# A hand-made planner for 32 graph batches: other landing times for tiles turned by DMA, and new seeds for its order

## The chip, the cores and the metric

The kernel runs on one core of one Trainium2 chip. The metric is the device time in microseconds (us) of one execution of the whole program; the median of several executions counts. The engines are called TensorE (PE; its weight loads are PEld), VectorE (DVE), ScalarE (ACT), GpSimd (POOL) and SyncE (SP). In this kernel SP issues all transfers.

## The reference

64 graphs of 256 nodes with 128 features, fp32, share one 256 x 256 matrix `adj`. Four layers follow each other; each is `x = layernorm(x + f(x))`:

```python
# layer 0, five times; in_matrix = out_matrix = adj
m  = adj @ h;  av = concat([m, m])
z  = sigmoid(av @ w3.T + w3_b + u3)         # u3 = h @ u3_w.T + u3_b
r  = sigmoid(av @ w4.T + w4_b + u3)
hv = tanh(av @ w5.T + w5_b + (r * h) @ u5.T + u5_b)
h  = (1 - z) * h + z * hv
# layer 1: A = masked softmax of edge values, split in diagonal and rest
out = (A * I) @ (x @ W0) + (A * (1 - I)) @ (x @ W1) + bias
# layer 2: attention scores s_src[i] + s_dst[j], leaky, masked by adj, softmax;
#          (attn * adj) @ h, layernorm, relu; then adj @ h_gat, two dense layers, relu
# layer 3: x, adj x, adj^2 x, adj^3 x, each times a weight, twice, summed
```

## The kernel before

**Work.** The 64 graphs go in 32 pairs (`n_pairs`). A pair's state is one tile of 128 partitions x 512 values (2 graphs x 2 halves of the nodes x 128). Each pair passes `layer0`, `layer1`, `layer2` and `layer3`; many pairs are under way at once. `spread7` multiplies by the adjacency with seven block products in place of eight, so that TensorE saves one in eight and VectorE and GpSimd make the sums (L632 to L647). Everything is fp32.

**Turning tiles.** A product needs its left factor transposed. Most tiles are turned by transfers and not by TensorE (`turn`, L559): VectorE transposes 32 x 32 blocks (L576); SP writes the tile to a scratch buffer in DRAM (L578, tile class E, 256 KB); four transfers bring it back with the blocks exchanged (L584, 64 KB each). `wide_turn` (L589 to L598) does the same with longer runs for the last step of layer 0. In `layer2` a line of scores is written to DRAM (L851) and read back to all partitions (L852). In layer 0 the tile `h` is turned after each of the five steps: L760 (candidate), L763 (tanh), L764, L765, L767 (new state), L576, L578, L584, then `spread7`'s sums (L632) and products (L626).

**Order.** The order of every queue is worked out by a planner in the kernel's own text, `Schedule`, at build time. Each operation is entered with `S.add`: the engines that can do it with a price in us each, what it reads and writes, and for a transfer a triple `dma = (wait, move, after)`. `order` (L162) is a list scheduler: of all ready operations it takes the one that can start first; ties go to the smaller due time `late`. It gives it the engine that would end first, and a tile of its class (`CLASSES`; 38 of A, 8 of E, 8 PSUM banks). For a transfer the modelled pipe moves on, and its result is seen `after` later:

```python
if op.dma:
    wait, move, after = op.dma
    moved = max(moved, end + wait) + move * MARGIN
    seen = moved + after - end + LAG
```

`Op.seen` (L110) also uses the sum of the triple, and with it `rest` and the due time. The emitted order is fixed; on the chip each engine goes through its queue in order, and semaphores hold an instruction until what it needs is there. A read of a turned tile at the head of SP's queue waits there for its write, and the transfers behind it wait with it.

**Seeds.** The time of the plan is cut into windows of 15 us (`WINDOW`). `SEEDS` has one whole number for each. Other than 0, it adds a small pseudo-random amount to the due times of all operations in that window (L188 to L191), and so decides between operations that could start at the same time.

**Buffers and last pairs.** Tiles come free when the planner reckons their last user done; the same landing times go into that (L216 to L220). The last pairs are planned with shorter due distances (`LAST_DUE`) and with more work on TensorE (`PLAIN`, `BY_DMA`), since fewer pairs are left to fill gaps.

Of the kernel before, what the change touches and what calls it, by code (L numbers as in the profile page):

```python
# [12 lines left out]
P = 128  # L13
# [45 lines left out]

XLOAD, TLOAD = (0.6, 1.33, 2.5), (0.6, 1.05, 1.5)  # L60

SEEDS = [0, 93, 322, 1448, 7531, 11255, 17694, 0, 22928, 0, 31333, 39097, 43244, 44818, 49258, 57598, 58877,
         63429, 68827, 73007, 78086, 84417, 87701, 93086, 94151, 102956, 104573, 109816, 0, 116864, 121863,
         126231, 131449, 135312, 139647, 0, 151536, 152814, 156731, 164059, 167161, 172217, 176318, 180425,
         187172, 188269, 195902, 197063, 202029, 208186, 213802, 218747, 223086, 224899, 230352, 233509, 240645,
         242828, 250716, 251650, 259527, 0, 0, 0, 0, 0, 283015, 0, 295474, 0, 0, 0, 0, 314335, 0, 322518, 0,
         333851, 338782, 340488, 345007, 350633, 356967, 37123594, 37124702, 37129757, 37131905, 37136837,
         37140404, 37142955, 37148792, 37152814, 37156664, 37159159, 37162334, 37167804, 37170295, 37173551, 0]


def mm(cols, n=1):
# [42 lines left out]
class Schedule:  # L114
# [47 lines left out]
    def order(self, tiles):  # L162
# [9 lines left out]
        while ready:  # L172
            best, homes, seed = None, {}, SEEDS[window] if window < len(SEEDS) else 0
            for op in ready:
# [64 lines left out]
def kernel(ctx: ExitStack, tc: tile.TileContext, x, xT, adj, adjT, mats, cols, rows, out):  # L239
    nc = tc.nc  # L240
# [5 lines left out]
    S = Schedule(n_pairs)  # L246
# [4 lines left out]
    def pe(us, fn, r, w):  # L251
        S.add([("PE", us, fn)], r, w)
# [4 lines left out]
    def dve(us, fn, r, w):  # L257
        S.add([("DVE", us, fn)], r, w)
# [11 lines left out]
    def evacuate(o, i, r, w, us=(0.49, 0.61)):  # L270

        S.add([("ACT", us[0], lambda: nc.scalar.copy(o(), i())),  # L272
               ("DVE", us[1], lambda: nc.vector.tensor_copy(o(), i()))], r, w)
# [271 lines left out]
    def tokens(v):  # L545
        return v.at(4, D)
# [6 lines left out]
    def by_dma(site):  # L553
        return S.pair < n_pairs - BY_DMA[site]
# [4 lines left out]
    def turn(i, name, site, n=512):  # L559


        o = Value("A", name=name) if n == 512 else i
        if not by_dma(site):
            ts = [Value("PS", name="ps") for _ in range(n // 512)]
            for k, t in enumerate(ts):
                def fn(k=k, t=t):
                    for c in range(4):
                        nc.tensor.transpose(tokens(t)[:, c, :], i.at(n // P, P)[:, 4 * k + c, :], ident.ap)
                pe(TURN, fn, [i, ident], [t])
            for k, t in enumerate(ts):  # L570
                evacuate(lambda k=k: o.at(n)[:, 512 * k:512 * k + 512], lambda t=t: t.at(512), [t], [o])
            return o
        st, d = Value("A" if n == 512 else "B", name="turn"), Value("E", name="turn")
        if site == "y":
            return wide_turn(i, st, d, o)
        dve(n / 512 * 0.55 + 0.09, lambda: nc.vector.transpose(st.at(n), i.at(n)), [i], [st])  # L576
        blocks = lambda *ap: bass.AP(tensor=d.ap.tensor, offset=d.ap.offset, ap=ap)
        S.add([("SP", 0.52, lambda: nc.sync.dma_start(blocks([P, P], [P * P, n // P], [1, P]), st.at(n // P, P)))],  # L578
              [st], [d], (0.6, n / 512 * 0.86, 0.5))

        def move():
            for q in range(4):
                b = blocks([P, 32], [32 * P, n // 32], [1, 32])
                nc.sync.dma_start(o.at(n // 32, 32)[32 * q:32 * q + 32],  # L584
                                  bass.AP(tensor=b.tensor, offset=b.offset + 32 * q, ap=b.ap))
        S.add([("SP", 2.1 if n == 512 else 2.7, move)], [d], [o], (-0.8, n / 512 * 1.5, 0.9))
        return o

    def wide_turn(i, st, d, o):  # L589

        line = lambda start, *ap: bass.AP(tensor=d.ap.tensor, offset=d.ap.offset + start, ap=ap)
        dve(0.64, lambda: nc.vector.transpose(st.at(4, 4, 32).rearrange("p q c e -> p c q e"), i.at(4, 4, 32)), [i], [st])
        S.add([("SP", 0.52, lambda: nc.sync.dma_start(line(0, [512, P], [1, 512]), st.at(512)))], [st], [d], (0.6, 0.63, 0.5))

        def move():
            for q in range(4):
                nc.sync.dma_start(o.at(4, P)[32 * q:32 * q + 32], line(P * q, [512, 32], [512 * 32, 4], [1, P]))
        S.add([("SP", 2.1, move)], [d], [o], (-0.8, 1.23, 0.9))  # L598
        o.turned = True
        return o  # L600

# [135 lines left out]
    def layer0(x0, hT):  # L737
        h = x0
        for s in range(STEPS):
# [18 lines left out]
            def candidate(t=t, mT=mT, r=r):  # L758
# [9 lines left out]
                new.at(512), t.at(512), 0.5, hT.at(512), op0=ALU.mult, op1=ALU.add), [t, hT], [new])  # L768
            hT = new
            h = turn(hT, "h", "h" if s < STEPS - 1 else "y")  # L770
        y = Value("A", name="y")
        halves = lambda v: v.at(4, 4, 32).rearrange("p s c e -> p c s e") if v.turned else v.at(4, 4, 32)
# [14 lines left out]
    def layer1b(x1):  # L787
        xT = turn(x1, "xT", "x1")
        xb, rr = Value("A", name="xb"), Value("A", name="rr")
        dve_or_pool(lambda e: e.tensor_add(tokens(xb), tokens(x1), row("l1_bias", 4)), [x1, rbc], [xb])  # L790
        ts = []
        for i in range(2):
            t = bank()

            def fn(i=i, t=t):
                for b in range(2):
                    nc.tensor.matmul(t.at(2, 2, D)[:, :, b, :], tokens(xT)[:, 2 * b + i, :], W1.ap[:, i_w:i_w + 2, :], start=(b == 0),  # L797
                                     stop=(b == 1), skip_group_check=True)
            pe(mm(256, 2), fn, [xT, W1], [t])
            evacuate(lambda i=i: rr.at(2, N)[:, i], lambda t=t: t.at(512)[:, N:], [t], [rr], (0.28, 0.34))  # L800
            part = lambda t=t: t.at(2, 2, D)[:, 0]
            dve(0.335, lambda i=i, part=part: nc.vector.scalar_tensor_tensor(
                part(), part(), dcol.ap[:, i:i + 1], xb.at(2, 2, D)[:, :, i, :], op0=ALU.mult, op1=ALU.add), [t, dcol, xb], [t])
            ts.append(t)
        for i, t in enumerate(ts):
            def fn(i=i, t=t):
                for j in range(2):
                    nc.tensor.matmul(t.at(512)[:, :N], offT.ap[:, j, i * P:(i + 1) * P], rr.at(2, N)[:, j],
                                     start=False, stop=(j == 1), skip_group_check=True)
            pe(mm(256, 2), fn, [offT, rr, t], [t])  # L810
        s, rs = scale_stats([(t, range(i, 4, 2)) for i, t in enumerate(ts)])
        for i, t in enumerate(ts):
            scale_tokens(t, x1, range(i, 4, 2), s, rs)

    def layer1(x1):
        if plain("q1"):
            return layer1b(x1)
        qT = spread7(x1, offT, offT7)
        xb = Value("A", name="xb")
        xd = Value("A", name="xd")  # L820
        dc = lambda: dcol.ap[:, None, :, None].to_broadcast([P, 2, 2, D])

        def scaled():
            for c in range(4):
                nc.scalar.mul(tokens(xd)[:, c, :], tokens(x1)[:, c, :], dcol.ap[:, c % 2:c % 2 + 1])
        S.add([("ACT", 1.26, scaled), ("DVE+", TT, lambda: nc.vector.tensor_mul(xd.at(2, 2, D), x1.at(2, 2, D), dc())),
               ("POOL", 1.235, lambda: nc.gpsimd.tensor_mul(xd.at(2, 2, D), x1.at(2, 2, D), dc()))], [x1, dcol], [xd])
        dT = turn(xd, "dT", "x1")
        dve_or_pool(lambda e: e.tensor_add(tokens(xb), tokens(x1), row("l1_bias", 4)), [x1, rbc], [xb])
        t = seed((0.49, 0.61), tokens, lambda: tokens(xb), [xb, qT, dT])  # L830
        scale_norm(products([qT, dT], [lambda: mat("l1w1"), lambda: mat("l1w0")], t), x1)

    def layer2(x2):
# [13 lines left out]
        srow, d, sd = Value("A", name="row"), Value("D", name="line"), Value("A", name="sd")  # L847
        u, s = Value("B", name="u"), Value("S", name="nm")
        line = lambda *ap: bass.AP(tensor=d.ap.tensor, offset=d.ap.offset, ap=ap)
        dve(0.25, lambda: nc.vector.transpose(srow.at(4, 32), hs()[:, :, D - 30:D + 2]), [h], [srow])  # L850
        S.add([("SP", 0.52, lambda: nc.sync.dma_start(line([32, 4], [P, 4], [1, 32]), srow.at(4, 32)[31::32]))], [srow], [d], (0.5, 0.1, 0.5))  # L851
        S.add([("SP", 0.52, lambda: nc.sync.dma_start(sd.at(512), line([0, P], [1, 512])))], [d], [sd], (0.9, 0.7, 1.2))  # L852

        nm, den = (lambda k=k: s.at(32)[:, 4 * k:4 * k + 4] for k in range(2))
        d2v = Value("S", name="d2")
# [278 lines left out]
```

## Time and profile before

| | |
|---|---|
| median of 3 runs | 1471.28 us (1470.71 to 1473.59) |
| the profiled execution: its time | 1470.14 us |
| its span, first to last instruction | 1468.4 us |
| mean granted TensorE clock | 0.999 |
| bytes read from HBM, written | 118.43 MB, 99.42 MB |
| transfers `e<-a` / `a<-e` (turned tiles) | 283 of 256 KB / 1132 of 64 KB |
| transfers `e<-b` / `b<-e` (attention weights) | 32 of 512 KB / 128 of 128 KB |

The page gives busy times and shares of the span, the busy share in 40 slices, the transfers, and the chain of work that ended last. A row of waits reads: the engine and line that waited, on whom, us in total, how often, the longest. A row of windows gives the stretch, its length, the busy us of PE, PEld, DVE, ACT and POOL (with the number of instructions), the clock, the share of time in which the DMA engines were busy, and GB/s. Tiles are named by class: `a` is a working tile in SBUF, `e` the scratch tile in DRAM, `ps` a PSUM bank.

### The profile page before, as it was taken

To read this page: it belongs to the slowest core of one execution; us is meant where nothing else is said; L and a number is where in the kernel's file an instruction comes from. 1 tells how busy PE (TensorE), PEld (TensorE's weight loads), DVE (VectorE), ACT (ScalarE), POOL (GpSimd) and SP (SyncE) were. 2 spreads that over 40 slices of the span, in tenths; PEclk is the share of its full clock that TensorE was granted. 3 is DMA by queue.
4 is the path that set the end of the run, shared out by engine and by line. 5 is a ranking of instruction groups with operands and counts; after the bars stand their busy time and mean duration, and the time that the engine had idled before them with its cause. 6 is when DMAs were issued, how large, how long until landed. Compare 5 with 4: busy or idle time off the path is not lost.

```text
span 1468.4 us, 29406 instructions
## 1 busy us (share of the span) xinstructions
PE 1457.9 (99%) x8188; PEld 1064.4 (72%) x8188; DVE 1270.8 (87%) x3161; ACT 1071.2 (73%) x3291; POOL 1005.7 (68%) x1551
## 2 busy tenths in 40 slices
PE   9999999999999999999999999999999999999998
PEld 6565666666677778777767777777777766788998
DVE  7877788888899999988888888888888999999995
ACT  3444555677788888778776778676786887789986
POOL 4532554566777889878766776777778786877664
PEclk9999999999999999999999999999999999999999
DMA  7553555767788988786767687676777695877773
GB/s 228 123 107 71 125 127 121 147 147 153 159 164 164 192 186 165 160 171 145 145 146 151 159 166 148 138 165 127 167 156 156 142 180 121 166 169 167 156 141 73
DMA packets 901284, 219.84 MB, mean 150 GB/s; under 512 B 673280, under 2 KB 892544, under 8 KB 901120
## 3 DMA queue, kind: packets, MB, share of 16 engines
q1 hardware_dynamic: 901120, 217.96, 71.1%
q8 instruction: 66, 1.08, 0.3%
q14 instruction: 98, 0.80, 0.2%
HBM read 118.43 MB, written 99.42 MB: 148 GB/s over the span
## 4 chain that ended last, share of the span: by engine, by line
PE 95%; DVE 2%; DMA 1%; ACT 1%; SPq 0%; issue 0%; POOL 0%; POOLq 0%; DVEq 0%; ACTq 0%
PE ps L626 24%; PE ps L744 9%; PE ps L745 9%; PE ps L752 9%; PE ps L759 9%; PE ps L760 9%; PE ps L782 7%; PE ps L1012 6%; PE ps L882 4%; PE ps L1055 2%; PE ps L842 2%; PE ps L608 2%; PE ps L1038 1%; PE ps L797 0%; DMA W<-mats_in 0%; SPq L584 0%
## 5 line engine op out<-in xcount | busy, mean ns | idle before, releaser
L626 PEld LDWEIGHTS ps<-aT,a 128*128 128x128 f32 x2192 | 296.4, 192 | 85.1 <-issue 74.8
L272 ACT COPY a<-ps 128x512 f32<-128x512 f32 (+2 forms) x610 | 255.1, 438 | 109.7 <-PE ps L626 53.1
L626 PE MATMUL ps<-aT,a 128*128 128x128 f32 x2192 | 321.3, 275 | 0.7 <-DVE a L632 0.7
L748 ACT ACTIVATE a<-ps,bzrh 128x512 f32<-128x512 f32 x160 | 110.5, 691 | 98.7 <-PE ps L745 94.7
L763 ACT ACTIVATE ps<-ps,bzrh 128x512 f32<-128x512 f32 x160 | 106.4, 665 | 96.6 <-PE ps L760 94.3
L759 PE MATMUL ps<-a,w 128*128 128x512 f32 x320 | 163.8, 593 | 0.0
L745 PE MATMUL ps<-a,w 128*128 128x512 f32 x320 | 163.4, 592 | 0.0
L760 PE MATMUL ps<-a,u5h 128*128 128x512 f32 x320 | 163.4, 592 | 0.0
L752 PE MATMUL ps<-a,w 128*128 128x512 f32 x320 | 163.3, 594 | 0.1
L647 DVE TENSOR_TENSOR a<-ps,a 128x256 f32<-128x256 f32 x237 | 98.5, 418 | 73.8 <-ACT a L272 50.5
L641 POOL TENSOR_TENSOR a<-a 128x256 f32<-128x256 f32 x125 | 93.1, 748 | 97.7 <-ACT a L272 96.7
L705 ACT ACTIVATE a<-ps 128x128 f32<-128x128 f32 x498 | 132.0, 289 | 36.2 <-PE ps L782 16.0
L713 POOL TENSOR_TENSOR s<-s,neg_half 128x4 f32<-128x4 f32 x127 | 140.2, 1105 | 6.8
L645 POOL TENSOR_TENSOR a<-a 128x128 f32<-128x128 f32 x204 | 100.6, 497 | 62.9 <-DVE a L641 52.9
L782 PEld LDWEIGHTS ps<-W,a 128*128 128x128 f32 x960 | 124.0, 192 | 18.0 <-issue 15.1
L754 ACT ACTIVATE a<-ps,bzrh 128x512 f32<-128x512 f32 x160 | 110.4, 692 | 36.4 <-PE ps L752 30.5
L782 PE MATMUL ps<-W,a 128*128 128x128 f32 x960 | 135.0, 275 | 0.0
L744 PE MATMUL ps<-a,W 128*128 128x512 f32 x256 | 131.0, 593 | 0.4 <-DVE a L647 0.4
L576 DVE STREAM_TRANSPOSE a<-a 128x512 f32<-128x512 f32 x185 | 128.3, 697 | 2.8 <-ACT a L705 0.5
L745 PEld LDWEIGHTS ps<-a,w 128*128 128x128 f32 x320 | 60.8, 190 | 76.5 <-issue 68.6
L760 PEld LDWEIGHTS ps<-a,u5h 128*128 128x128 f32 x320 | 60.8, 190 | 76.5 <-issue 64.8
L725 ACT ACTIVATE a<-ps,s 128x128 f32<-128x128 f32 x362 | 109.0, 388 | 5.0 <-POOL s L713 3.5
(266 smaller groups left out, 3612.7 us busy)
## 6 DMA issues: line engine op xcount, KB each, us to landing
e<-a SPq DMA_DIRECT2D x283, 256.0 KB
a<-e SPq DMA_DIRECT2D x1132, 64.0 KB
e<-b SPq DMA_DIRECT2D x32, 512.0 KB
b<-e SPq DMA_DIRECT2D x128, 128.0 KB
x<-x_in SPq DMA_DIRECT2D x32, 256.0 KB
t<-xT_in SPq DMA_DIRECT2D x32, 256.0 KB
a<-d SPq DMA_DIRECT2D x32, 256.0 KB
y_out<-a SPq DMA_DIRECT2D x31, 256.0 KB
```

The source lines that it names most:

```text
L272: S.add([("ACT", us[0], lambda: nc.scalar.copy(o(), i())), ("DVE", us[1], lambda: nc.vector.tensor_copy(o(), i()))], r, w)
L576: dve(n / 512 * 0.55 + 0.09, lambda: nc.vector.transpose(st.at(n), i.at(n)), [i], [st])
L626: pe(mm(128), lambda: nc.tensor.matmul(blk(t, k), left(), rt(), start=start, stop=True, skip_group_check=True), [*r, right, terms, *[t] * ...
L705: nc.scalar.activation(tokens(junk)[:, c, :], v.at(len(tiles), D)[:, k, :], AF.Square, scale=D ** -0.5, accum_out=mv()[:, c, 1:2])
L713: pool(1.02, lambda: nc.gpsimd.tensor_tensor(rs(), rs(), neg_half.ap, op=ALU.pow), [s, neg_half], [s])
L744: nc.tensor.matmul(t.at(512), mat("u3"), hT.at(512), start=True, stop=False)
L745: nc.tensor.matmul(t.at(512), w4.ap, mT.at(512), start=False, stop=True)
L748: act(0.59, lambda t=t, r=r: nc.scalar.activation(r.at(512), t.at(512), AF.Tanh, bias=bzrh.ap[:, 1:2], scale=0.5), [t, bzrh], [r])
L752: pe(mm(512), lambda t=t, mT=mT: nc.tensor.matmul(t.at(512), w3.ap, mT.at(512), start=False, stop=True, skip_group_check=True), [w3, mT, t ...
L759: nc.tensor.matmul(t.at(512), w5.ap, mT.at(512), start=True, stop=False)
L760: nc.tensor.matmul(t.at(512), u5h.ap, r.at(512), start=False, stop=True)
L782: nc.tensor.matmul(tokens(t)[:, c, :], tokens(i)[:, c, :], w(), start=(first and k == c == 0), stop=(k == len(lefts) - 1), skip_group_chec ...
```

## The change

The landing times of the turned tiles become four numbers of one tuple, all larger than before, and the table of seeds is a new one. No operation, engine choice or price is edited otherwise.

```diff
+SLOW = (1.3, 1.1, 1.4, 0.8)
+
-SEEDS = [0, 93, 322, 1448, 7531, 11255, 17694, 0, 22928, 0, 31333, 39097, 43244, 44818, 49258, 57598, 58877,
...
+SEEDS = [0, 113, 303, 1481, 0, 12107, 0, 23552, 32642, 38944, 40117, 45598, 51141, 55839, 63359, 69543, 72829,
...
         S.add([("SP", 0.52, lambda: nc.sync.dma_start(blocks([P, P], [P * P, n // P], [1, P]), st.at(n // P, P)))],
-              [st], [d], (0.6, n / 512 * 0.86, 0.5))
+              [st], [d], (0.6, n / 512 * 0.86, SLOW[0]))
...
-        S.add([("SP", 2.1 if n == 512 else 2.7, move)], [d], [o], (-0.8, n / 512 * 1.5, 0.9))
+        S.add([("SP", 2.1 if n == 512 else 2.7, move)], [d], [o], (-0.8, n / 512 * 1.5, SLOW[1]))
...
-        S.add([("SP", 0.52, lambda: nc.sync.dma_start(line(0, [512, P], [1, 512]), st.at(512)))], [st], [d], (0.6, 0.63, 0.5))
+        S.add([("SP", 0.52, lambda: nc.sync.dma_start(line(0, [512, P], [1, 512]), st.at(512)))], [st], [d], (0.6, 0.63, SLOW[0]))
...
-        S.add([("SP", 2.1, move)], [d], [o], (-0.8, 1.23, 0.9))
+        S.add([("SP", 2.1, move)], [d], [o], (-0.8, 1.23, SLOW[1]))
...
-        S.add([("SP", 0.52, lambda: nc.sync.dma_start(line([32, 4], [P, 4], [1, 32]), srow.at(4, 32)[31::32]))], [srow], [d], (0.5, 0.1, 0.5))
-        S.add([("SP", 0.52, lambda: nc.sync.dma_start(sd.at(512), line([0, P], [1, 512])))], [d], [sd], (0.9, 0.7, 1.2))
+        S.add([("SP", 0.52, lambda: nc.sync.dma_start(line([32, 4], [P, 4], [1, 32]), srow.at(4, 32)[31::32]))], [srow], [d], (0.5, 0.1, SLOW[3]))
+        S.add([("SP", 0.52, lambda: nc.sync.dma_start(sd.at(512), line([0, P], [1, 512])))], [d], [sd], (0.9, 0.7, SLOW[2]))
```

Since the planner works the whole order out anew from these numbers, the queues of all engines differ from about the 28th microsecond of TensorE's work on; the first 44 operations of TensorE and its last 15 are the same. Lines of the kernel after are two higher than before from `SLOW` on.

## The prediction

> **What bounds the kernel now.** I read the page first (shares, slices, chain), then the waits of TensorE, then windows of the late stage, then what SP's queue waits for.
>
> The page:
>
> ```profile
> span 1468.4 us, 29406 instructions
> PE 1457.9 (99%) x8188; PEld 1064.4 (72%) x8188; DVE 1270.8 (87%) x3161; ACT 1071.2 (73%) x3291; POOL 1005.7 (68%) x1551
> ...
> DVE  7877788888899999988888888888888999999995
> ...
> q1 hardware_dynamic: 901120, 217.96, 71.1%
> ...
> PE 95%; DVE 2%; DMA 1%; ACT 1%; SPq 0%; issue 0%; POOL 0%; POOLq 0%; DVEq 0%; ACTq 0%
> ```
>
> TensorE is busy 99% and is 95% of the chain that ended last. The other 5% of the chain is not idle TensorE: the chain passes through other engines while TensorE still works off its queue. What TensorE itself waited for, in the view of waits:
>
> ```profile
> PE ps L1012 <- DVE a L901: 1.4, 1, 1.4
> PE ps L332 <- DVE ones L330: 1.2, 1, 1.2
> PE ps L842 <- DMA a<-e: 0.8, 1, 0.8
> PE ps L626 <- DVE a L632: 0.7, 1, 0.7
> PE ps L808 <- DVE ps L802: 0.4, 1, 0.4
> PE ps L744 <- DVE a L647: 0.4, 1, 0.4
> PE ps L1012 <- ACT x L725: 0.2, 1, 0.2
> ```
>
> Seven stops, each once, 5.1 us in all. Only one ends with a DMA. By the timeline the 1.2 and the 0.7 belong to the start; the other five lie at 1193, 1304, 1326, 1357 and 1368 us. The windows say the same (us, PE, PEld, DVE, ACT, POOL, clock, DMA share, GB/s):
>
> ```profile
> 12.00:480.00 468.00, 468.00 (x2214) 304.01 (x2213) 393.51 (x870) 294.36 (x754) 264.81 (x417) 1.00 0.65 139
> 480.00:1160.00 680.00, 680.00 (x3959) 500.68 (x3959) 596.24 (x1512) 522.97 (x1626) 515.72 (x797) 1.00 0.75 156
> 1160.00:1200.00 40.00, 39.50 (x269) 32.18 (x268) 37.67 (x93) 30.49 (x107) 32.40 (x48) 1.00 0.91 173
> 1280.00:1320.00 40.00, 39.16 (x246) 31.57 (x245) 36.05 (x96) 33.98 (x123) 31.33 (x48) 1.00 0.71 155
> 1320.00:1360.00 40.00, 39.39 (x277) 35.25 (x276) 39.76 (x123) 36.81 (x147) 32.28 (x47) 1.00 0.75 163
> 1360.00:1400.00 40.00, 38.52 (x276) 36.29 (x275) 37.54 (x118) 36.49 (x149) 26.98 (x37) 1.00 0.77 165
> ```
>
> For 1148 us TensorE never stops; later it loses bits where VectorE is at 90 to 99%.
>
> A busy PE need not be at its pitch, so I priced it. In the timeline 128-column matmuls start 0.112 us apart (16 in 1.79), 256-column ones 0.216, 512-column ones 0.429. The records hold 6028 + 256 of the first kind (130 columns with them), some 290 of the second, 1600 of the third: 704 + 63 + 686 = 1453 us. So 15 us of the span are not matmul at pitch: about 4.6 up to the 12th us, 5.3 after the last matmul starts (1463.1), and 5.2 between. Those 5.2 are the 3.2 that the waits show, about 0.26 hidden in each of five stops (a matmul is drawn 0.275 long and starts 0.112 apart, and the first after a stop is 0.1 late), and two short gaps that only the chain shows (1171, 1370 us).
>
> What SP's queue waits for:
>
> ```profile
> SPq L578 <- DVE a L576: 142.0, 83, 8.0
> SPq L584 <- DMA e<-a: 115.9, 83, 4.7
> ...
> SPq L597 <- DMA e<-a: 21.9, 17, 2.9
> SPq L584 <- DMA e<-b: 18.0, 12, 3.2
> ...
> SPq L852 <- DMA d<-a: 3.7, 4, 1.1
> ```
>
> A read of a turned tile waits at the head of SP for its write 112 times, 156 us in all; every later transfer stands behind it. That is what the change works on.
>
> [...]
>
> **The change part by part.** No instruction of TensorE or SP is added or removed: 4110 matmuls as the program issues them (the fp32 ones appear as two in the records) and the same 1744 transfers, shape by shape. So the 1453 us and the 218 MB stay. Three things move.
>
> (a) *The planner's landings.* Write 0.5 to 1.3, read 0.9 to 1.1, line write 0.5 to 0.8, line read 1.2 to 1.4 us. They change only when an operation counts as ready. In the two orders, of 347 write/read pairs, those with nothing between on SP go from 39 to 19, one operation 106 to 88, two 94 to 114, three 55 to 73; the mean from 2.11 to 2.28. A filler read issues four transfers at about 0.49 (L584), 2 us of cover. Twenty pairs out of zero, at the 1.4 us of a mean wait (115.9/83), is some 28 us less waiting of SP, a fifth of 156. Its worth for the end: what TensorE loses to transfers, 0.83 + 0.26 = 1.1 us at 1304. Nothing else, since TensorE's own queue covers the rest.
>
> (b) *Room on TensorE.* Counting matmuls at pitch between the one a turned h hangs on (L760) and the first that needs it (L626): least 13.1 us before, 13.7 after; twentieth part 14.5 and 15.4; median 21.8 and 24.4. The chain itself is 0.665 + 0.688 + 0.684 + 0.678 + 0.697 (L763 to L576) + 2.8 landing of the write + three issues at 0.49 + 4.3 of the last read = 12.0. The tightest gain 0.6 us. Before 1160 us this is worth nothing.
>
> (c) *New seeds reshuffle everything from the 28th us on.* By counts, VectorE gets 11 more 128x512 TENSOR_TENSOR (0.69 us each), 5 more 128x256 (0.42), 4 more 128x512 scalar forms (0.5), and gives up 4 statistics pairs (0.4), 2 copies, some small ones: +8 us. ScalarE loses 16 128x128 (0.4) and 4 512-wide (0.6): -8. GpSimd loses 11 128x512 (1.3) and gains 6 128x256 (0.75) and 3 128x128 (0.5): -8. Spread over the span these cost nothing under TensorE; beside its last 300 us VectorE has as many operations in the planner's list (553 before, 555 after). In the stage where TensorE's work passes from 1320 to 1360 us, GpSimd goes from 46 operations to 54 (two L710/L713 pairs at 1.39, five at 0.75, less one at 0.5): 32.3 + 6.0 = 38.3 of 40 us, while VectorE falls from 86 to 79. That is a bottleneck exchanged for another: bounded below by -1.15 (what TensorE loses there now: 0.19 + 0.42 + two hidden parts) and above by +6 if all of GpSimd's addition shows. I take +0.6, since GpSimd still fits and VectorE is relieved. The start (first 44 operations of TensorE) and the last 15 are the same, so 4.6 and 5.3 stay.
>
> Sum: 1468.4 - 1.1 (a) + 0.6 (c), other late gaps taken as exchanged one for one = 1467.9. The profiled execution took 1470.14, 1.7 more than its span; the median is 1471.28, 1.1 above that. So 1470.8.
>
> **Rivals.**
> *Likeliest: same within 0.2%* (0.2% is 2.9 us, about what a measurement can tell). TensorE's late idle stays between 2.5 and 8 us: 1468.5 to 1474. For it: pitch, unchanged matmuls, 1148 us without a stop. Against: all late stops are chance meetings of queues and are drawn anew. Chance 0.44.
> *Transfers were behind the late stops too.* The stops that end at VectorE would go back to tiles that landed late, and the new room would remove nearly all 5.2: 1471.28 - 4.5 = 1466.8. For it: DMA share 0.91 at 1160, 14 stops of GpSimd's L632 at a<-e (26.8 us). Against: four of five end at VectorE or ScalarE, 90 to 99% busy. No version of this order can get below 1466. Chance 0.20.
> *Slower: the late crowd.* Place: 1320 to 1400 us, the last 14 batches ending together. Price: GpSimd's +6.0 us of work in a stage with 7.7 us of room; its L713 lies in each normalisation, nothing else can run it, and L705/L725 on ScalarE and then TensorE wait. It decides once GpSimd's queue passes 40 us of work in 40, so with 1.7 us of waits on top; then 1471.28 + 5 = 1476. For it: VectorE was at 39.76 of 40 there. Chance 0.28.
> *The change doesn't do what it says*: delayed reads push loads and later writes back, SP (1004 issues of L584's small reads alone take 0.487 us each, 489 us) meets the same waits elsewhere, and several late tiles come 2 to 4 us late: 1480. For it: fillers load the DMA engines in between. Against: distances grew on average. Chance 0.08.
>
> **How the numbers follow.** Faster by over 0.2% 0.20, within 0.44, slower 0.36. Range: from 1466.8, the floor of the second case, to 1478, past the crowd; outside stay most of the last case and a bad crowd. The likeliest one's own range is 1468.5 to 1474.
>
> **What would show it.** (a) right: L584 and L597 waiting for e<-a and e<-b fall from 156 to about 125 us and no TensorE stop ends with a DMA. (b) right: no TensorE stop from 12 to 1160 us. (c) right: late windows lose 2 to 8 us of TensorE; GpSimd near 38 us at 1320. The forecast is wrong if windows before 1160 show TensorE under full, or if TensorE's late idle is under 2 or over 8 us.

## The result, and the profile after

The kernel after takes 1468.98 us (median of 19, 1468.22 to 1470.28), the kernel before beside it 1471.15 (median of 19, 1469.49 to 1473.59): ratio 0.9985, 95% interval 0.9978 to 0.9992. That is 2.2 us or 0.15% less: real by the interval, and inside the 0.2% that was called no change.

The page of after (busy us, share of the span, instructions; then the transfers):

```profile
span 1468.5 us, 29324 instructions
PE 1458.2 (99%) x8188; PEld 1064.8 (73%) x8188; DVE 1277.1 (87%) x3166; ACT 1067.8 (73%) x3277; POOL 990.8 (67%) x1549
...
q1 hardware_dynamic: 901120, 217.96, 70.9%
```

TensorE is as full as before. VectorE has 6.3 us more work, ScalarE 3.4 and GpSimd 14.9 less. What TensorE waited for, after:

```profile
PE ps L1014 <- POOL a L634: 1.6, 1, 1.6
PE ps L628 <- DVE a L634: 1.3, 2, 0.7
PE ps L334 <- DVE ones L332: 1.2, 1, 1.2
PE ps L746 <- DVE a L649: 0.5, 1, 0.5
PE ps L628 <- DMA a<-e: 0.3, 1, 0.3
```

4.9 us in place of 5.1, in other places. The windows of after (PE, PEld, DVE, ACT, POOL busy) answer to those of before:

```profile
480.00:1160.00 680.00, 678.58 (x3978) 502.19 (x3977) 606.11 (x1524) 522.17 (x1631) 507.63 (x786) 1.00 0.77 158
1160.00:1200.00 40.00, 39.90 (x205) 26.96 (x204) 38.03 (x94) 32.50 (x91) 25.85 (x43) 1.00 0.77 152
...
1280.00:1320.00 40.00, 40.00 (x266) 32.14 (x265) 36.63 (x99) 36.45 (x124) 33.65 (x50) 1.00 0.84 165
1320.00:1360.00 40.00, 39.94 (x281) 35.97 (x280) 38.85 (x122) 37.62 (x153) 37.34 (x53) 1.00 0.76 167
1360.00:1400.00 40.00, 38.35 (x272) 36.04 (x271) 37.04 (x116) 36.84 (x144) 28.07 (x37) 1.00 0.79 156
```

From 1160 us on TensorE now loses 1.8 us where it lost 3.4; but it loses 1.4 between 480 and 1160, where before lost nothing. So the two profiled spans are level (1468.4 and 1468.5), and the 2.2 us of the medians are not to be seen in this pair of profiles: before's profiled execution (1470.14 us) was quicker than 16 of the 19 times of before, and after's (1470.28 us) was the slowest of its 19.

What did change plainly is SP's queue. Its waits for the writes of turned tiles and of the score line, after:

```profile
SPq L586 <- DMA e<-a: 52.3, 39, 3.5
...
SPq L586 <- DMA e<-b: 15.3, 9, 3.3
...
SPq L599 <- DMA e<-a: 12.1, 6, 3.9
...
SPq L854 <- DMA d<-a: 8.6, 8, 2.3
```

88 us in 62 waits, against 160 us in 116 before.

### The profile page after: what moved, and what is told of

It reads as the page before. It is cut to its first block, busy times and chain, and to the rows that moved or that the text cites. A ratio compares the mean times of both kernels' runs of the same rounds, so it can differ in the third digit from the quotient of the medians.

```text
span 1468.5 us, 29324 instructions
## 1 busy us (share of the span) xinstructions
PE 1458.2 (99%) x8188; PEld 1064.8 (73%) x8188; DVE 1277.1 (87%) x3166; ACT 1067.8 (73%) x3277; POOL 990.8 (67%) x1549
## 4 chain that ended last, share of the span: by engine, by line
PE 94%; DVE 2%; POOL 2%; SPq 1%; issue 1%; DMA 0%; ACT 0%; POOLq 0%; DVEq 0%; ACTq 0%
PE ps L628 24%; PE ps L761 9%; PE ps L746 9%; PE ps L762 9%; PE ps L747 9%; PE ps L754 9%; PE ps L784 7%; PE ps L1014 6%; PE ps L884 4%; PE ps L1057 2%; PE ps L844 2%; PE ps L610 1%; PE ps L1040 1%; SPq L586 1%; PE ps L799 0%
## 5 line engine op out<-in xcount | busy, mean ns | idle before, releaser
L274 ACT COPY a<-ps 128x128 f32<-128x128 f32 (+2 forms) x612 | 255.7, 437 | 112.0 <-PE ps L628 52.2
L643 POOL TENSOR_TENSOR a<-a 128x256 f32<-128x256 f32 x139 | 107.2, 774 | 93.1 <-ACT a L274 90.4
L746 PE MATMUL ps<-a,W 128*128 128x512 f32 x256 | 131.1, 594 | 0.5 <-DVE a L649 0.5
L767 DVE SCALAR_TENSOR_TENSOR ps<-a,ps 128x512 f32<-128x512 f32 x160 | 109.2, 683 | 3.8 <-ACT a L756 2.8
```

The source lines that it names most:

```text
L274: S.add([("ACT", us[0], lambda: nc.scalar.copy(o(), i())), ("DVE", us[1], lambda: nc.vector.tensor_copy(o(), i()))], r, w)
L746: nc.tensor.matmul(t.at(512), mat("u3"), hT.at(512), start=True, stop=False)
```

## The experiments

Twelve kernels, in three sets. Two questions: did the landing times bring the 2.2 us, or the new seeds; and do TensorE's stops hang on transfers at all? Where the kernel before is given beside a set, it ran on the same chip.

**Landings and seeds apart** (e1 to e4).

```diff
 e1: -SLOW = (1.3, 1.1, 1.4, 0.8)
     +SLOW = (0.5, 0.9, 1.2, 0.5)      # seeds of after kept
 e2: seeds of before, SLOW of after
 e3: SLOW as in e1,  SEEDS = [0]
 e4: SLOW of after,  SEEDS = [0]
```

> The landing times of before with the seeds of after. If the landings themselves bring the gain, this is at the time of before, 1471 us or a little more. If the new seeds bring it, it is at 1469. If a table of seeds only fits the landings it was made with, it is above both kernels, 1473 or more, and SP waits for its writes about 160 us as before.

> The landing times of after with the seeds of before. Landings: 1469 us, with SP's waits for writes near 90 us. Seeds: 1471. A misfit of the two: 1473 or more, though SP's waits fall all the same.

> No seeds at all, landing times of before. By the landings theory this is slower than its partner with the landing times of after by 2 us or more. By the seeds theory both are the same and both slower than the seeded kernels by several us (1473 to 1485).

> No seeds, landing times of after. Landings theory: 2 us or more below the partner with the landing times of before. Seeds theory: level with it, 1473 to 1485. In both, SP waits for writes about half as long as in the partner.

Measured, beside a before of 1470.86: e1 1507.46 (ratio 1.0244, 1.0230 to 1.0258), e2 1500.94 (1.0207, 1.0193 to 1.0221), e3 1505.79 (1.0244, 1.0227 to 1.0262), e4 1496.68 (1.0174, 1.0160 to 1.0188).

All four are 26 to 37 us slower than the kernel before. I had expected a misfit to cost 2 us; it costs as much as having no seeds at all. A table of seeds is worth its 2% only with the landing times that it stands beside; by the planner's text, other landing times change what is ready at each moment, so that a window begins from another state. The planner's own reckoning shows the loss too: worked out again from the kernels' text, its plan (`self.span`) ends at 1481 us for before and 1482 for after, but between 1513 and 1540 for e1 to e4, e11 and e12. So these orders are worse already as plans. (Among the six, and between before and after, the plan's end doesn't rank the measured times.) The change can't be divided into "landings" and "seeds" by these runs; it is a pair exchanged for a pair. Without fitting seeds the larger landings look worth 9 us (e3 to e4), and 6.5 across e1 and e2. The last set tests that.

Where e3 and e4 lose their time (stretches 12 to 1280, 1280 to 1440 us, and 1440 us to the end of the span at 1503.8 and 1495.7; columns as above), first e3, then e4:

```profile
12.00:1280.00 1268.00, 1260.45 (x6812) 886.65 (x6811) 1116.32 (x2636) 885.19 (x2600) 851.09 (x1345) 1.00 0.71 148
1280.00:1440.00 160.00, 153.81 (x1020) 134.21 (x1019) 142.45 (x429) 128.19 (x485) 123.87 (x184) 0.98 0.80 155
1440.00:1520.00 80.00, 47.59 (x326) 44.16 (x324) 32.34 (x95) 32.56 (x135) 23.45 (x37) 0.90 0.23 50
```

```profile
12.00:1280.00 1268.00, 1262.75 (x6769) 883.81 (x6768) 1105.21 (x2606) 870.67 (x2539) 859.37 (x1352) 1.00 0.71 147
1280.00:1440.00 160.00, 146.97 (x1002) 130.16 (x1001) 144.13 (x433) 138.41 (x554) 123.59 (x177) 0.98 0.80 162
1440.00:1520.00 80.00, 50.18 (x387) 48.21 (x385) 33.04 (x96) 38.97 (x155) 29.26 (x47) 0.98 0.22 50
```

In 1268 us TensorE loses 8 us (e3) and 5 (e4); in the next 160 alone 6 and 13; after 1440 us e3 loses 16 more and e4 5.5. In the kernel before these stretches lose 0.5, 3 and 5 us. So most of the idle time that these two orders add lies in the last part, where few pairs are left. The rest of their loss, 14 and 12 us, is drawn as busy: 1461.9 and 1459.9 us in these stretches, against 1447.9 in before.

**Profiles again, and reads that wait for nothing** (e5 to e8).

```diff
 e5, e6: no edit
 e7 (of before), e8 (of after):
+        cold = x.offset + S.pair % 16 * 131072
-                                  bass.AP(tensor=b.tensor, offset=b.offset + 32 * q, ap=b.ap))
+                                  bass.AP(tensor=x.tensor, offset=cold + 32 * q, ap=b.ap))
...
```

> A second profile of the kernel before. In its first one the span was 1468.4 us, as short as that of after (1468.5), while the medians differ by 2.2 us. If the first profile was a lucky execution, this one shows TensorE stops that the first had not, ending with transfers (landings theory) or with VectorE and ScalarE (chance meetings), 1 to 4 us more in all.

> A second profile of the kernel after, whose first profile was the longest of its 19 times. A span of about 1467 us is expected, with the stops of 558 and 570 us smaller or gone if they were chance, there again if the order itself makes them.

> The kernel before, in the same order, but the reads of turned tiles fetch parts of the input x instead of what was written, so that no read waits for its write; the turned values are left out. If late writes are what before loses against after, this runs at the time of after or below, 1466 to 1469 us, without a TensorE stop that ends with a transfer. If its stops come from VectorE and ScalarE alone, it stays at 1470 to 1471.

> The kernel after, edited in the same way. Here little should be left to gain: 1467 to 1469 us. If it drops as much as before does under the same edit, the landings were not what the change cured; if it comes down to the same time as before with free reads, they were all of it.

e5: 1468.58 us, span 1466.8. What TensorE waited for in it:

```profile
PE ps L1012 <- DVE a L901: 1.4, 1, 1.4
PE ps L332 <- DVE ones L330: 1.2, 1, 1.2
PE ps L744 <- DVE a L647: 0.5, 1, 0.5
PE ps L808 <- DVE ps L802: 0.4, 1, 0.4
PE ps L1012 <- ACT x L725: 0.2, 1, 0.2
```

The same stops as in the first profile, at the same instructions, with the same lengths, but the one that ended with a transfer (0.8 us, L842) is gone, and so is the small start stop. So four of the five late stops belong to the order (they stand in the profiles of e7 and e9 too), and one was chance. My expectation of more stops in a second profile was a miss: this execution is shorter still.

e6: 1470.04 us, span 1468.3. The 1.6 (L1014) and the 0.5 (L746) are there again, and the stop of 570 us too, here of 0.38:

```profile
569.01 0.71 PE L628 MATMUL ps<-offT,a 128*128 128x128 f32 x4 [0.38 <-DVE a L634]
```

The stop of 558 us is gone; a new one of 0.5 stands at 1277, which e8 and e10 have as well. Again order and chance side by side; the expected span of 1467 was missed too.

Beside a before of 1471.20: e7 1469.98 us (13 runs), ratio 0.9992 (0.9984 to 1.0); e8 1468.29 us (11 runs), ratio 0.9979 (0.9970 to 0.9988). SP's waits for writes fall from 160 to 6 us in e7 and from 88 to 9 in e8; what is left is mostly the score line's. The time of e7 lies between those that the two theories gave it, that of e8 is as expected. Waiting for writes thus costs before about 1.2 us, and its interval just reaches none at all. After stands at 0.9985 with the wait and at 0.9979 without it: 0.9 us, and the intervals overlap. So a gap between the two stays, about 1.7 us by these medians, and late *writes* are not what makes it. (The edit also moves the reads to other addresses in DRAM; that was not tried apart.)

**No chain waits for a turned h** (e9, e10). To the edit of e7 and e8 this adds that products and sums take h from the tile that it was turned from; the transfers still run.

```diff
+        self.instead = None
...
-        t = self.ap[:, :n]
+        t = (self if own or self.instead is None else self.instead).ap[:, :n]
...
             h = turn(hT, "h", "h" if s < STEPS - 1 else "y")
+            h.instead = hT if s < STEPS - 1 else None
```

> The kernel before, same order, with free reads and, in the first four steps of layer 0, products and sums that take h from the unturned tile, so that no part of layer 0's chain waits for a transfer of h; the turning of h is left out of what is computed, all transfers still run. If the 1.7 us that stay between before and after with free reads come from late landings of reads, this falls to 1468 or below, level with its partner. If they come from the queues of VectorE, ScalarE and GpSimd, it stays at 1469.5 to 1470 and the gap stays.

> The kernel after, edited in the same way: 1467.5 to 1468.5 by either theory; the gap to its partner decides. Level: read landings made the difference. Still 1.5 us or more below the partner: the compute queues did.

Beside a before of 1470.24: e9 1469.26 us (ratio 0.9994, 0.9985 to 1.0002), e10 1469.94 (0.9995, 0.9986 to 1.0003). The unedited before had been at 1471.20 on this same chip beside e7 and e8, so comparisons between the two sets are unsure by about 1 us. The two are level, as the theory of late reads had it, but not in its manner, and both expected times were missed: before hardly moved from e7 (0.9992) while after rose from 0.9979 to 0.9995. An edit that should only take waits away made after, if anything, slower. TensorE's waits in e10 don't explain it; they come to 4.0 us, against 4.3 in e8 and 4.9 in after:

```profile
PE ps L1021 <- POOL a L640: 1.6, 1, 1.6
PE ps L335 <- DVE ones L333: 1.2, 1, 1.2
PE ps L817 <- DVE ps L811: 0.5, 1, 0.5
PE ps L891 <- DMA b<-x_in: 0.4, 1, 0.4
PE ps L806 <- DVE a L642: 0.3, 1, 0.3
```

The stops of 570 and 1158 us are gone (1158 was gone in e8 already), so by these profiles, one of each kernel, they hang on turned tiles; others (L891, L806) have come. In e9 all four of before's own stops remain:

```profile
PE ps L1019 <- DVE a L908: 1.4, 1, 1.4
PE ps L333 <- DVE ones L331: 1.2, 1, 1.2
PE ps L750 <- DVE a L653: 0.7, 1, 0.7
PE ps L815 <- DVE ps L809: 0.4, 1, 0.4
PE ps L1019 <- ACT x L731: 0.2, 1, 0.2
```

So these four (1.4, 0.7, 0.4, 0.2; the 1.2 is the start) hang neither on SP's waits for the writes of turned tiles nor on the first four h of layer 0. The reads of the other turned tiles still land and are still waited for in e9, so transfers aren't ruled out altogether. In these profiles, then, before's order-made stops end at VectorE and ScalarE, and after has exchanged part of them for two that do hang on turned tiles. The chain of waits of after shows the one at 570 (start us, us, what):

```profile
556.63 2.10 DMA a<-e
...
558.80 0.74 POOL a L634
559.54 1.44 POOL s L670
...
568.64 1.46 DVE a L634
570.10 0.04 issue
570.14 0.71 PE ps L628 x4
```

A tile lands at 558.7. TensorE itself waits 0.3 us for a landing just then; the chain goes on through the queues of GpSimd and VectorE, and TensorE, which has other work queued, stops for it again 11 us later. In e6 and e8 the first of these stops is gone and the second is still there, with 0.4 us.

**Writes alone, reads alone** (e11, e12), both without seeds.

```diff
 e11: SLOW = (1.3, 0.9, 1.2, 0.5)
 e12: SLOW = (0.5, 1.1, 1.4, 0.8)
```

> No seeds; only the landing of the big writes is raised (1.3), the reads and the score line stay as in before. If the write's landing carries the gain of the two unseeded kernels (1505.8 to 1496.7), this is at 1496 to 1499 and SP's waits for writes are near 90 us; if the reads carry it, it is at 1503 to 1506.

> No seeds; only the reads and the score line are raised (1.1, 1.4, 0.8), the big write stays at 0.5. If the writes carry the gain: 1503 to 1506 with SP's waits for writes near 200 us. If any larger landing helps: 1498 to 1501. If each such edit is a new draw of the order, writes alone and reads alone will not add up to the 9 us.

Beside the same before of 1470.24: e11 1520.24 us (ratio 1.0337, 1.0322 to 1.0352), e12 1509.62 (1.0262, 1.0248 to 1.0277). By the ratios, raising one half alone costs 14 us (writes) or 3 us (reads) against e3; both halves together gain 9 to 10. The two halves don't add up to the whole, which is what was expected if each edit is a new draw of the order; neither time itself was expected. SP's waits for writes do follow the write's landing (in e1, e2 and e11 they are some 30 us longer than expected), and the time doesn't follow them:

| | e3 | e12 | e1 | before | e2 | e11 | e4 | after |
|---|---|---|---|---|---|---|---|---|
| SP's waits for writes, us | 240 | 188 | 191 | 160 | 119 | 120 | 104 | 88 |
| ratio to before | 1.0244 | 1.0262 | 1.0244 | 1 | 1.0207 | 1.0337 | 1.0174 | 0.9985 |

What most of the slow kernels share is a late entry of the last pair. The loads of x, in the view of that tile (duration least/median/most in ns; first to last start, us), of before, after, e11 and e4:

```profile
L297 SPq DMA_DIRECT2D x<-x_in x32: 367/442/3568, 1.2 to 1183.5; - x32
```

```profile
L299 SPq DMA_DIRECT2D x<-x_in x32: 367/452/3200, 1.2 to 1174.8; - x32
```

```profile
L293 SPq DMA_DIRECT2D x<-x_in x32: 368/444/3726, 1.2 to 1235.4; - x32
```

```profile
L293 SPq DMA_DIRECT2D x<-x_in x32: 367/446/3205, 1.2 to 1140.2; - x32
```

In e1, e2, e3 and e12 the last load starts at 1218 to 1233 us, and these end 271 to 283 us later, e11 283 us later. Before and after leave it 285 and 294 us. No last pair here is through in less than 271 us; if that is about what one needs (an estimate from these eight profiles), one that enters at 1235 can't be out by 1470. e4, with the earliest last load, is the fastest of the unseeded ones, and loses by something else (13 us of TensorE between 1280 and 1440). That late entry is the cause was not tried by itself; it is what all the slow orders but one have in common.

No edited kernel that does the whole computation beats the kernel after.

## Why the prediction was right, and where it was not

**The bound: right.** At the pitch measured in before the matmuls come to 1453 us, and every profile here holds the same 8188 records of them; since start and end stay as they were, before's profiled execution had little but its 5 us of late idle for another order to gain. The forecast of no change followed from that and holds: the gain is 2.2 us.

**(a) The transfers: right in kind, too small by a factor of 2.7.** SP's waits for the writes of turned tiles were to fall by 28 us, from 156 to about 125; they fell by 76, to 80 (with the score line from 160 to 88). The step that failed is the price "twenty pairs out of zero at 1.4 us". The waits of the two traces, sorted by how many of SP's operations the planner has put between a write and its read (score line included), show why; pairs with four or more between never wait:

| operations between | 0 | 1 | 2 | 3 |
|---|---|---|---|---|
| before: pairs, of them waiting, us | 39, 39, 86 | 106, 51, 54 | 94, 23, 18 | 55, 4, 3 |
| after: pairs, of them waiting, us | 19, 19, 41 | 88, 25, 34 | 114, 13, 11 | 73, 5, 2 |

A pair with nothing between waits 2.2 us, not the mean 1.4, so those twenty alone gave 45 us of the 72; nearly all of the other 27 came from pairs with one or two operations between, which the forecast had left out. The worth for the end was put at 1.1 us; e7 measures 1.2 for all write waits of before. That agreement is luck: the 1.1 was read from the stop at 1304 us, which e5 shows to be chance. (The 2.8 us that the prediction counts in (b) for the landing of a write come from a single one: in before SP began to issue it at 1292.77 us and it landed 2.82 us on. From 1294.66 us until then SP issued nothing; the read behind it went out at 1295.61. Why this landing took that long was not shown.)

**(b) Room on TensorE: wrong by its own sign.** No stop was to come between 12 and 1160 us; after has 1.4 us of them, and windows before 1160 us under full were named as a sign of a wrong forecast. The least room (13.7 us) was counted for h alone and from matmul to matmul; it does not see that GpSimd's and VectorE's queues stand in between, as the chain at 570 shows.

**(c) The late crowd: right in load, off in effect.** Over the whole span VectorE was to gain 8 us of work and ScalarE and GpSimd to lose 8 each; measured are +6.3, -3.4 and -14.9. GpSimd in 1320 to 1360 us was put at 38.3 us and measured 37.34. TensorE was to lose 0.6 more there; it lost 0.06 in all, so 0.55 less than before, and 1.65 in place of 1.48 in the next window. The slower rival's trigger (40 us of work in 40) was not reached.

**The sum.** The span was put at 1467.9; measured 1468.5 and 1468.3. That it came so near is partly luck: by the windows TensorE lost 1.6 us less after 1160 us, where the sum had 0.5 less, and 1.4 more before 1160, for which the sum had nothing. The mis-sized term of the median is the last one, from a profiled execution to the median: taken as +1.1 from before's one profile. For after it is -1.3 and -1.1 (1470.28 and 1470.04 profiled, 1468.98 median). The first of these is 2.4 us off; less the 0.6 us by which the span was put too short, that is the 1.8 us between 1470.8 and 1468.98.

**The rivals.** "Transfers were behind the late stops too" is not borne out: its 1466.8 us was not reached, and all four late order-made stops of before survive e9, in which, however, only the h of four steps is free of its reads. "The change doesn't do what it says" falls: SP's waits are halved. "The late crowd" did not decide.

**What stays open.** Where the 2.2 us come from. Of the 19 times of before 11 are over 1471 us, of after none; with free reads 1 of 13 of before's, with free h none of 13. That points to late tiles that hit before's order in some executions, but weakly: the unedited before was over 1471 us 13 times of 23 beside e7, and only 5 times of 24 beside e9. Such drifts of about 1 us are as large as what the edits do, e10 rose where it should not have, and the profiled executions of before (1470.14 and 1468.58) are both below its median and show no such stop but one. No profile has caught the slower execution.

## What to carry to other kernels

When one engine is full from end to end, count its work at pitch first: the rest is the most that any reordering can bring, however long the waits elsewhere are; here the rest was 15 us of 1468.4, some 10 of them at the start and the end, and SP's waits fell by 72 us while the time fell by 2. A fitted table (seeds, an order, offsets) belongs to the exact model that it fits: change a constant of the model alone and the fit is lost, so compare fitted with fitted, and don't read a constant's worth from unfitted draws. Ask the model first: here the end of its own plan told the two fitted orders from the six others. In a pipeline of many items, look also at when the last one enters.

## What the runs showed that I had not expected

One constant of a planner moved by 0.8 us changes the time of an unseeded order by 14 us (e3 to e11), against a spread of 1 us among e11's own four runs. The starved end shows more than its stops. In e11 the granted TensorE clock was 0.82 between 1440 and 1480 us and 0.59 from 1480 to 1500, and in these two stretches TensorE stood still for up to 6.9 us at a time; most matmuls of 128 columns took 0.37 us from 1480 to 1510 us against 0.275 from 1400 to 1440 us, where the clock was 1.00. How the stops, the lower clock and the longer matmuls hang together was not tried. In the two tuned kernels no late stop is longer than 1.6 us and the clock stays at 1.00 up to 1440.
